# One Haar product in split float32r form for all 64 channels of the second batch instead of every other one

## The chip, the cores and the metric

The kernel runs on one core of one Trainium2 chip. The metric is the device time of one execution in microseconds (us), taken as the median of several runs. Engines are named as in the profile: PE is TensorE's matmul, PEld its weight load, DVE is VectorE, ACT is ScalarE, SP is SyncE, whose queue issues most of the DMAs.

## What is computed

The input x has 4 batches of 64 channels of 256x256 float32 pixels. Four layers follow one another. Layers 0, 1 and 3 are long convolutions, each with its own separable filter made by a small network; layer 2 is a Haar transform in two dimensions, a mixing over channels with soft thresholds, and the inverse transform.

```python
# layers 0, 1, 3
k = jnp.einsum('ijk,imk->ijmk', hx, hy)[0]          # separable filter of each channel
y = irfft2(rfft2(x) * rfft2(k) / fft_size)[..., :L, :L]
out = y + x * bias[:, None, None]
# layer 2
f1 = haar2d(x)
for i in range(2):
    f4 = jnp.einsum('bchw,oc->bohw', f1 * v[i], conv_w[i])
    acc = acc + jnp.sign(f4) * jax.nn.relu(jnp.abs(f4) - tau[i])
y = haar2d(acc, inverse=True) + x
```

## The kernel before

**Convolutions as triangular matrix products.** The filters are separable, so each convolution of a 256x256 image is a product with a Toeplitz matrix along the columns and one along the rows. `toeplitz` loads such a matrix from a padded row of the filter in DRAM. `contract` (lines 189 and 190) does one side of one channel: for each of the two halves of 128 output rows one 128x256 and one 128x128 float32 matmul (a product with a zero quarter left out). `first` runs it and copies the PSUM result out on ACT (line 198, tiles `pa` to `a`); `second` runs the other side and adds the bias term on DVE (line 211, tiles `py` to `y`).

**Haar transform along the rows and down the columns.** After layer 1 a channel lies in `sd`, a ring of 8 channels. `pairs` and `levels` do the transform along the rows on DVE (lines 256, 257, 266, 267), `levels` for 4 channels at once in three steps. `down` does the transform down the columns as one product with a 128x128 matrix of Haar signs on PE, giving tile `pz`; ACT copies it to `co` (line 293) and SP stores it in DRAM (`coef`). There are two forms of `down`:

- Plain: one float32 product of `hbt` with the channel's `sd`, 512 columns (line 289).
- In parts, for channels in `in_parts`: `split` rounds the channel to float32r on ACT (line 277) and subtracts the rounded values on DVE (line 278), so that the two float32r tiles in `sp` add up to the channel. `down` then does two float32r products with `hbr` into the same PSUM bank (line 285). The matrix holds only signs[...]. `sp` has one buffer.

**Mixing and the way back.** `mixing` works on 64 groups of 4 rows of coefficients. Per group: four float32 products 128x256 (line 334, tile `px`, two PSUM buffers of two banks); the scale v on the way out of PSUM, for all but the last batch 4 of 16 slices on DVE (line 351) and 12 on ACT (line 353); absolute value and sign on ACT (lines 359, 360); threshold, product and sum on DVE (lines 361, 366, 370). `inverse` does the inverse transforms (`rows`, `cols`, lines 387 to 415) and layer 3's convolution for two channels out of three. The rest are put off and run by `convolution` beside the last batch's mixing.

**Order.** Nothing runs at once: every stage of every channel or group is put on a list with a tick (`at`, `stream`), the list is sorted, and the instructions are emitted in this order. A scheduler then gives each engine its own order, which it follows strictly. The convolutions of batch b+1 run beside the mixing and the inverse of batch b: `spread` deals 64 channels over the ticks, so that some ticks have a channel and some have none. For the second batch (b+1 = 1) these are ticks 64 to 145, with 64 channels; for the third and fourth batch the channels lie closer, 64 in 72 ticks. Ticks with no channel are called empty below. In the mixing of the first batch they come every four or five ticks (15 while its 64 groups run), in that of the second batch every nine (7 while its groups run).

`convolutions` gets `in_parts` as a range. Batches 0, 2 and 3 have all channels in it, batch 1 every other one.

Of the kernel before, what the change touches and what calls it, by code (L numbers as in the profile page):

```python
# [16 lines left out]
B, C, S, EMB, ORD = 4, 64, 256, 33, 64  # L17
# [20 lines left out]
def conv_seq_kernel(ctx, tc, x, fz, fw, bias, decay, haar, haar_row, factors, vt, taut, wmix, out):  # L38
# [138 lines left out]
    def toeplitz(layer, c, name):  # L177

        t = tp.tile([P, 2, S], F32, name=name, tag="toep")
        nc.sync.dma_start(t, ap(pads[layer], c * 2 * ROW, [[1, P], [ROW, 2], [1, S]]))  # L180
        return t

    def bank(name):
        return psm.tile([P, 2, S], F32, name=name, tag="mm")
# [7 lines left out]
    def first(b, st, key, layer, new):  # L192
        def run(c):
            s = st[c]
            ps = bank(f"p{new}_{b}_{c}")
            contract(ps, s[key], s[layer][:, 0, :])
            a = io.tile([P, 2, S], F32, name=f"{new}_{b}_{c}", tag="mid")
            nc.scalar.copy(a, ps)  # L198
            s[new] = a

        return run

    def second(b, st, key, layer, res, new, tag, ahead=None):
        def run(c):
            s = st[c]
            if ahead is not None:
                s[ahead] = toeplitz(ahead, c, f"t{ahead}_{b}_{c}")
            ps = bank(f"p{new}_{b}_{c}")
            contract(ps, s[key], s[layer][:, 1, :])
            y = io.tile([P, 2, S], F32, name=f"{new}_{b}_{c}", tag=tag, bufs=BUFS[tag])  # L210
            nc.vector.scalar_tensor_tensor(y, s[res], bsb[:, layer, c : c + 1], ps, ALU.mult, ALU.add)  # L211
            s[new] = y

        return run
# [12 lines left out]
    def at(tick, place, run, unit):  # L227
        events.append((tick, place, len(events), run, unit))

    def stream(stages, ticks):  # L230

        for unit, tick in enumerate(ticks):
            for s, stage in enumerate(stages):
                if stage is not None:
                    at(tick + s, -s, stage, unit)

    def convolutions(b, ticks, in_parts=(), border=None):


        st = {}  # L240

        def after(tick, n):
            return tick if border is None or tick < border or n < C // 4 - 2 else border + 3 * (tick - border)

        def load(c):
            xt = io.tile([P, 2, S], F32, name=f"x_{b}_{c}", tag="in", bufs=3)
            nc.sync.dma_start(xt, x[b, c].rearrange("(k p) w -> p k w", p=P))
            st[c] = {"x": xt, 0: toeplitz(0, c, f"t0_{b}_{c}")}

        last_second = second(b, st, "a1", 1, "y0", "y1", "res")  # L250

        def pairs(c):
            last_second(c)
            v = st.pop(c)["y1"].rearrange("p k (w e) -> p k w e", e=2)
            t = sd[:, c % 8]
            nc.vector.tensor_add(t[:, :, 0, :], v[:, :, :, 0], v[:, :, :, 1])
            nc.vector.tensor_sub(t[:, :, 1, :], v[:, :, :, 0], v[:, :, :, 1])
            nc.scalar.dma_start(keep[b][c], t)

        def levels(steps):  # L260
            def run(n):
                t = sd[:, n % 2 * 4 : n % 2 * 4 + 4]
                for step in steps:
                    v = t[:, :, :, 0, :].rearrange("p c k (w e) -> p (c k) w e", e=2 * step)
                    even, odd = v[:, :, :, 0], v[:, :, :, step]
                    nc.vector.tensor_sub(odd, even, odd)  # L266
                    nc.vector.scalar_tensor_tensor(even, even, 2.0, odd, ALU.mult, ALU.subtract)  # L267

            return run

        parts = {}

        def split(c):

            w = parts[c] = mx.tile([P, 2, 2, S], F32R, name=f"sp_{b}_{c}", tag="sp", bufs=1)
            t = sd[:, c % 8].rearrange("p k e w -> p k (e w)")
            nc.scalar.copy(w[:, 0], t)  # L277
            nc.vector.tensor_tensor(w[:, 1], t, w[:, 0].bitcast(F32), ALU.subtract)  # L278

        def down(c):  # L280
            ps = bank(f"pz_{b}_{c}")
            flat = "p k w -> p (k w)"
            if c in in_parts:
                for i in range(2):
                    nc.tensor.matmul(
                        ps.rearrange(flat), hbr, parts[c][:, i].rearrange(flat), start=(i == 0), stop=(i == 1)
                    )
            else:
                nc.tensor.matmul(
                    ps.rearrange(flat), hbt, sd[:, c % 8].rearrange("p k e w -> p (k e w)"), start=True, stop=True  # L290
                )
            t = io.tile([P, 2, S], F32, name=f"co_{b}_{c}", tag="co", bufs=BUFS["co"])
            nc.scalar.copy(t, ps)
            nc.sync.dma_start(coef[b][:, c].rearrange("k p w -> p k w"), t)

        stream(
            [load, first(b, st, "x", 0, "a0"), second(b, st, "a0", 0, "x", "y0", "y", ahead=1), first(b, st, "y0", 1, "a1"), pairs],
            ticks,
        )
        for n in range(C // 4):  # L300
            end = ticks[4 * n + 3] + 4
            for s, steps in enumerate([(1,), (2, 4), (8, 16, 32, 64)]):
                at(after(end + 1 + s, n), 1, levels(steps), n)
            for j in range(4):
                if 4 * n + j in in_parts:
                    at(after(end + 3 + j, n), 2, split, 4 * n + j)
                at(after(end + 4 + j, n), 2, down, 4 * n + j)
        return after(ticks[-1] + 11, C // 4 - 1)
# [128 lines left out]
    def convolution(which, ticks):  # L437

        for (b, c), tick in zip(which, ticks):
            st = {}  # L440

            def load(c, b=b, st=st):
                u = io.tile([P, 2, S], F32, name=f"v_{b}_{c}", tag="in", bufs=3)
                nc.sync.dma_start(u, late[b, c])
                st[c] = {"u": u, 2: toeplitz(2, c, f"t2_{b}_{c}")}

            for s, stage in enumerate([load, *last(b, st)]):
                at(tick + s, -s, stage, c)


    def spread(begin, end, n=C):
        return [begin + i * (end - begin - 1) // (n - 1) for i in range(n)]
# [19 lines left out]
    ready = convolutions(0, range(C), in_parts=range(C))  # L472
    ahead = C
    start = ready + 3
    for b in range(B):
        mixing(b, start, 12 if b + 1 < B else 6)
        end = start + groups + 3
        if b + 1 < B:
            ready = convolutions(b + 1, spread(ahead, end + 2), in_parts=range(0, C, 2 if b == 0 else 1), border=end)
        else:  # L480
            convolution(
                [(i, c) for i in range(B - 1) for c in sorted(put_off)], spread(start - 2, end + 2, (B - 1) * len(put_off))
            )
        inverse(b, end, put_off if b + 1 < B else ())

        start = max(end + C, ready + 3)
        ahead = start - 3
# [111 lines left out]
```

## Time and profile before

| | |
|---|---|
| runs (us) | 2994.05, 2999.53, 2990.19; median 2994.05 |
| profiled execution | 2994.63 us, its span 2992.8 us |
| PE busy | 2929.2 us, 98% of the span, 16950 instructions |
| PEld busy | 2610.1 us, 87% |
| DVE busy | 2535.0 us, 85% |
| ACT busy | 2147.1 us, 72% |
| TensorE clock granted | full in all 40 slices |
| DMA | 649.72 MB, mean 217 GB/s |

Read by the first and last `px` product, the stretches of the span are: filters and convolutions of the first batch up to 452 us; mixing of the first batch beside convolutions of the second, 452 to 867; inverse of the first beside the rest of the second's convolutions, 867 to 1094; the same two stretches for the next batch, 1094 to 1543 and 1543 to 1774, and the next, 1774 to 2222 and 2222 to 2452; the last mixing, 2452 to 2729, and its inverse to the end. Busy time counts an instruction from its start to its end as recorded; instructions of one engine overlap somewhat, and a float32 matmul of the program stands in the trace as two instructions.

### The profile page before, as it was taken

The page shows a single profiled execution, that of the slowest core. Times are in us where ns is not written, and L with a number is a line of the kernel's source. Part 1 is how long each engine was busy: PE and PEld are TensorE (multiplying, and loading weights), DVE is VectorE, ACT ScalarE, POOL GpSimd, SP SyncE. Part 2 cuts the span into 40 slices and gives each one's busy share as a digit, 9 for nine tenths or more (in the row PEclk, how much of TensorE's full clock was granted, in tenths as well). Part 3 has the DMA queues.
Part 4 walks back from the last instruction along what each step waited for, and adds up shares of the span by engine and source line. Part 5 has one row for each costly group of instructions (what it writes and reads, how often), then busy time and mean ns, then how long its engine had stood idle before and what let it go on. Part 6 is the DMA issues. An engine that isn't in the chain of part 4 may idle for free. (4 is left out here: it accounts for less than half of the span.)

```text
span 2992.8 us, 51867 instructions
## 1 busy us (share of the span) xinstructions
PE 2929.2 (98%) x16950; PEld 2610.1 (87%) x16950; DVE 2535.0 (85%) x4544; ACT 2147.1 (72%) x4973; POOL 0.2 (0%) x4
## 2 busy tenths in 40 slices
PE   7999999999999999999999999999999999999999
PEld 6899988888888888888888988888888988888998
DVE  4766778999988879999989879999998889998776
ACT  1333337989876658889886658989886768887554
POOL 0000000000000000000000000000000000000000
PEclk9999999999999999999999999999999999999999
DMA  5877776676667876666677876676677887777776
GB/s 146 250 233 230 229 232 207 206 206 199 204 196 245 247 216 202 206 210 201 207 212 241 253 222 198 209 212 202 205 210 234 254 239 229 229 233 220 211 212 186
DMA packets 562496, 649.72 MB, mean 217 GB/s; under 512 B 44369, under 2 KB 447412, under 8 KB 562100
## 3 DMA queue, kind: packets, MB, share of 16 engines
q1 hardware_dynamic: 446132, 494.94, 57.9%
q10 hardware_dynamic: 116096, 151.46, 14.1%
q8 instruction: 137, 2.24, 0.3%
q14 instruction: 131, 1.07, 0.1%
HBM read 426.77 MB, written 219.48 MB: 216 GB/s over the span
## 5 line engine op out<-in xcount | busy, mean ns | idle before, releaser
L189 PE MATMUL py<-t,a 128*128 128x256 f32 x3072 | 923.1, 382 | 19.2 <-ACT a L198 12.3
L198 ACT COPY a<-pa 128x512 f32<-128x512 f32 x768 | 472.4, 617 | 440.6 <-PE pa L190 305.7
L190 PEld LDWEIGHTS py<-t,a 128*128 128x128 f32 x3072 | 583.4, 190 | 79.3
L353 ACT ACTIVATE f<-px,vt 128x64 f32<-128x64 f32 x2688 | 588.8, 351 | 87.7 <-DVE f L351 81.8
L190 PE MATMUL py<-t,a 128*128 128x128 f32 x3072 | 590.1, 274 | 0.0
L189 PEld LDWEIGHTS py<-t,a 128*128 128x128 f32 x3072 | 491.0, 191 | 78.2 <-ACT a L198 35.7
L334 PE MATMUL px<-wb,f 128*128 128x256 f32 x2048 | 503.5, 381 | 16.7 <-ACT f L353 16.7
L334 PEld LDWEIGHTS px<-wb,f 128*128 128x128 f32 x2048 | 362.6, 191 | 62.1 <-ACT f L353 26.7
L361 DVE TENSOR_TENSOR mag<-mag,vt 128x1024 f32<-128x1024 f32 x256 | 312.2, 1220 | 30.9 <-ACT mag L359 28.8
L366 DVE SCALAR_TENSOR_TENSOR mag<-mag,f 128x1024 f32<-128x1024 f32 x256 | 311.9, 1218 | 3.8 <-DVE sd L267 0.3
L397 ACT CAST w<-pw 128x512 fp32r<-128x512 f32 x256 | 150.4, 587 | 227.9 <-PE pw L395 215.1
L189 PE MATMUL pa<-t,y 128*128 128x256 f32 x1024 | 306.9, 382 | 1.7 <-DVE y L211 1.4
L189 PE MATMUL pa<-t,x 128*128 128x256 f32 x1024 | 305.6, 380 | 1.3 <-issue 1.3
L359 ACT ACTIVATE mag<-f 128x1024 f32<-128x1024 f32 x256 | 284.3, 1110 | 18.7 <-DVE z L370 6.8
L387 ACT COPY zc<-z 128x512 f32<-128x512 f32 x256 | 282.4, 1103 | 2.0 <-ACT w L397 0.8
L360 ACT ACTIVATE f<-f 128x1024 f32<-128x1024 f32 x256 | 274.0, 1070 | 12.1 <-DVE sd L266 5.9
L211 DVE SCALAR_TENSOR_TENSOR y<-x,bsb,py 128x512 f32<-128x512 f32 x256 | 190.3, 743 | 57.8 <-PE py L190 49.9
L189 PE MATMUL pa<-t,u 128*128 128x256 f32 x772 | 232.8, 383 | 3.2 <-PE pu L407 3.2
L411 DVE SCALAR_TENSOR_TENSOR t<-r,pu 128x512 f32<-128x512 f32 x256 | 175.1, 684 | 64.1 <-PE pu L407 60.6
L278 DVE TENSOR_TENSOR sp<-sd,sp 128x512 fp32r<-128x512 f32 x224 | 153.9, 687 | 83.0 <-ACT sp L277 81.3
L190 PEld LDWEIGHTS pa<-t,x 128*128 128x128 f32 x1024 | 194.6, 190 | 26.3
L190 PEld LDWEIGHTS pa<-t,y 128*128 128x128 f32 x1024 | 194.5, 190 | 26.3
(67 smaller groups left out, 4449.0 us busy)
## 6 DMA issues: line engine op xcount, KB each, us to landing
t<-pad SPq DMA_DIRECT2D x768, 256.0 KB, 4.0
x<-in_x SPq DMA_DIRECT2D x256, 256.0 KB, 3.9
keep<-sd ACTq DMA_DIRECT2D x256, 256.0 KB, 3.0
coef<-co SPq DMA_DIRECT2D x256, 256.0 KB, 3.2
f<-coef SPq DMA_DIRECT2D x256, 256.0 KB, 4.0
r<-keep SPq DMA_DIRECT2D x256, 256.0 KB, 3.3
out_y<-y ACTq DMA_DIRECT2D x256, 256.0 KB, 3.7
late<-u ACTq DMA_DIRECT2D x63, 256.0 KB, 2.7
```

The source lines that it names most:

```text
L189: nc.tensor.matmul(ps[:, m, :], src[:, 0, m * P : (m + 1) * P], t[:, ::-1], start=True, stop=False)
L190: nc.tensor.matmul(ps[:, m, P:], src[:, 1, m * P : (m + 1) * P], t[:, : P - 1 : -1], start=False, stop=True)
L198: nc.scalar.copy(a, ps)
L211: nc.vector.scalar_tensor_tensor(y, s[res], bsb[:, layer, c : c + 1], ps, ALU.mult, ALU.add)
L334: nc.tensor.matmul(ps[:, h, q, :], f[:, q, h * P : (h + 1) * P], wb.rearrange("p r n -> p (r n)"), start=True, stop=True,)
L353: nc.scalar.mul(f4[:, j], px[:, j], scale(g, 0)[:, j : j + 1])
L359: nc.scalar.activation(mag, f4, AF.Abs)
L360: nc.scalar.activation(f4, f4, AF.Sign)
L361: nc.vector.tensor_sub(mag, mag, over(g, 1, 16))
L366: nc.vector.scalar_tensor_tensor(mag, mag, 0.0, st[g]["f4"], ALU.max, ALU.mult)
L387: nc.scalar.copy(a, z[:, :, :, c].rearrange("p h (i k) -> p h k i", k=2))
L411: nc.vector.scalar_tensor_tensor(t, st[c]["r"], 0.5, ps, ALU.mult, ALU.add)
```

## The change

The second batch's channels all go in parts: `in_parts` becomes `range(C)` for every batch. For 32 channels (the odd ones of the second batch) the plain product is replaced by a split and two float32r products. The branch for the plain form stays in the code but is not used any more.

```diff
@@ -476,7 +476,7 @@
         mixing(b, start, 12 if b + 1 < B else 6)
         end = start + groups + 3
         if b + 1 < B:
-            ready = convolutions(b + 1, spread(ahead, end + 2), in_parts=range(0, C, 2 if b == 0 else 1), border=end)
+            ready = convolutions(b + 1, spread(ahead, end + 2), in_parts=range(C), border=end)
         else:
             convolution(
                 [(i, c) for i in range(B - 1) for c in sorted(put_off)], spread(start - 2, end + 2, (B - 1) * len(put_off))
```

The parts of `convolutions` that the choice steers:

```python
        def split(c):
            w = parts[c] = mx.tile([P, 2, 2, S], F32R, name=f"sp_{b}_{c}", tag="sp", bufs=1)
            t = sd[:, c % 8].rearrange("p k e w -> p k (e w)")
            nc.scalar.copy(w[:, 0], t)
            nc.vector.tensor_tensor(w[:, 1], t, w[:, 0].bitcast(F32), ALU.subtract)
...
                if 4 * n + j in in_parts:
                    at(after(end + 3 + j, n), 2, split, 4 * n + j)
                at(after(end + 4 + j, n), 2, down, 4 * n + j)
```

## The prediction

> **What bounds the kernel now.** I read the page's busy shares first, then busy time by stretch, the two forms of the product `pz`, the matmul starts in the timeline, and who waits for whom. The page:
>
> ```profile
> PE 2929.2 (98%) x16950; PEld 2610.1 (87%) x16950; DVE 2535.0 (85%) x4544; ACT 2147.1 (72%) x4973; POOL 0.2 (0%) x4
> ```
>
> PE looks full. Since matmuls overlap in the record, I took the start-to-start spacing: in steady rows a float32 256-column instruction starts 0.216 us after the one before, a 128-column one after 0.110. Whatever exceeds the usual spacing of the same pair of lines I call lost; it is 10.8 us in the first mixing stretch, 14.3 in the second, 13.8 in the third, 11.1 in the last. So PE bounds every stretch, with 2 to 4% lost. Busy time by stretch (first, second, last mixing; the columns after the length are PE, PEld, DVE, ACT):
>
> ```profile
> 452.00:867.00 415.00, 409.32 (x2210) 354.94 (x2209) 377.60 (x654) 368.99 (x1055) 0.00 (x0) 1.00 0.68 204
> 1094.00:1543.00 449.00, 440.62 (x2456) 391.96 (x2454) 411.32 (x718) 389.29 (x1094) 0.00 (x0) 1.00 0.68 205
> 2452.00:2729.00 277.00, 272.21 (x1461) 239.86 (x1461) 268.85 (x316) 235.20 (x558) 0.00 (x0) 1.00 0.79 231
> ```
>
> The reader is to see that VectorE (91%) and ScalarE (89%) are close behind PE in the stretch where the change adds to both.
>
> The waits in the first and, in the second fence, the second mixing stretch:
>
> ```profile
> PE px L334 <- ACT f L353: 2.2, 3, 1.1
> ```
>
> ```profile
> PE px L334 <- ACT f L353: 5.1, 7, 0.8
> ```
>
> In the second stretch, where every channel goes in parts already, PE stops seven times for ScalarE to empty a `px` buffer: once for each of its seven empty ticks.
>
> **What the Trainium skill says.** "Perfetto Trace Analysis", section Identifying the Most-Contended Engine, warns that matmul busy share is no good measure and points to weight loads; here these are 87%, and the spacing decides. "TensorE: Matmul & The Clock Gate", section Back-to-back issue gap, gives N/2.4 + 2.5 ns, 216 ns for 512 columns. The trace agrees for one recorded float32 instruction only if it is counted as two passes (256 columns in 216 ns, 512 in 430). For float32r the trace has 0.314 and 0.233 us for the two products of 512 columns, more than the page's 0.216, so I use the trace. "VectorE: DVE Perf Modes", section The TRN2 errata, gives (N+151)/0.96, 691 ns, for a float32 `tensor_tensor` of 512; the subtraction of line 278 takes 687, and back to back the next starts after 0.60.
>
> **The change part by part.**
>
> *1. Cheaper products, 32 of them.* Plain form, then form in parts, each with what PE starts next:
>
> ```profile
> 603.48 1.02 PE L289 MATMUL pz<-sd,hbt 128*128 128x512 f32 x2
> ...
> 604.34 0.59 PE L189 MATMUL py<-t,a 128*128 128x256 f32 x2
> ```
>
> ```profile
> 1287.91 0.71 PE L285 MATMUL pz<-sp,hbr 128*128 128x512 f32 x2
> 1288.46 0.59 PE L189 MATMUL pa<-t,y 128*128 128x256 f32 x2
> ```
>
> PE is held 0.86 us in one, 0.55 in the other. The medians over all rows give 0.431 + 0.430 = 0.861 against 0.314 + 0.233 = 0.547: 0.314 us a channel. All 32 plain products lie between 452.7 and 1009.5 us; line 289 has 50 instructions, so 25 channels, in the first mixing stretch and 14, so 7 channels, in the inverse behind it. **PE's own work falls by 25 x 0.314 = 7.8 and 7 x 0.314 = 2.2, together 10.0 us.** Weight loads stay two a channel.
>
> *2. 32 splits.* Each is a cast on ScalarE (0.52 us when the next follows at once: starts 1290.95 and 1291.47) and a subtraction on VectorE (0.60: starts 1292.50 and 1293.10). In the first mixing that is 25 x 0.52 = 13.0 us and 25 x 0.60 = 15.0. It is hidden only while these engines stay ahead of PE. Over the shortened 415 - 7.8 = 407 us VectorE would have (377.6 + 15.0) / 407 = 96% and ScalarE (369.0 + 13.0) / 407 = 94%. The last mixing runs at 97% of VectorE and loses 11.1 of 277 us. In the inverse stretch VectorE has 186.6 of 227 us, and 7 splits there cost nothing: PE's work covers them, and were this cover gone they would cost at most 7 x 0.60 = 4.2.
>
> *3. Waits added.* `sp` has one buffer, so the cast for one channel waits for both products of the channel before, now one tick earlier instead of two; behind it on ScalarE stand the `px` copies and the `pa` copies, for which PE waits. In 224 splits now, 192 of them with the next channel split too, no cast is listed as waiting for `pz`; 0 us. The casts wait for VectorE's line 267 (4.8 us, six times), and the products for no subtraction of line 278. I take 0; lower bound 0, since no wait is removed, upper bound 25 x 0.2 us (those six waits average 0.8, one in four) = 5. DMAs are the same in number and size; SP's order differs in a few places, whose waits I take as nothing, within ±1 us.
>
> *4. The order.* In the built program of the changed kernel PE's order outside the second batch's convolutions stays as it was, inside it does not. In the second mixing each empty tick makes a knot: the `px` of one group directly followed by the first half of the next group's. Seven knots there; the timeline at one:
>
> ```profile
> 1281.72 1.89 PE L334 MATMUL px<-wb,f 128*128 128x256 f32 x8
> 1284.41 1.13 PE L334 MATMUL px<-wb,f 128*128 128x256 f32 x4 [0.80 <-ACT f L353]
> ```
>
> The line shows PE standing until ScalarE has emptied the older buffer. Such a knot loses 0.96 + 0.10 there and 0.25 + 0.07 + 0.32 + 0.10 within the next 21 us, 1.8 us in all. The first mixing has six knots now, one in its start-up; the other five lose 0.3, 0.7, 0.2, 1.1 and 0.9 us, 0.64 each. **In the changed program it has fourteen, one at nearly each empty tick.** The 10.8 us lost now are 2.4 at the start-up (to 480 us), 3.2 at five knots, 5.2 at smaller stops around other empty ticks, which the new knots replace. After: 2.4 + 14 x s. With s = 0.64 (knots of this stretch) 11.4; with s = 1.8 (knots with all channels split, but nine ticks apart) 27.6. I choose 1.2, the middle: the same splits as there, but in a looser knot (the changed order has mostly 4.9 + 4.9 + 1.7 us of PE work between the four `px` starts, the second mixing's 4.9 + 4.3 + 1.7). That is 19.2 us, 8.4 more than now; bounds +0.6 and +16.8.
>
> *Sum.* -10.0 + 0 + 0 + 8.4 = **-1.6 us** against the profiled execution's own 2994.6 (span 2992.8 and 1.8 around it), so 2993.0. The median of the runs is 0.6 below that execution: **2992.5 us**. With both ends of s, -9.4 to +6.8, with the cast's wait up to +12. A measurement of this kernel can tell about 0.3%, 9 us, from no change, so even the whole gain of 10.0 would hardly show.
>
> **The rivals.**
>
> *A. The full 10 us.* The knots cost no more than the stops that they replace, and ScalarE and VectorE keep ahead: 2994.05 - 10 = 2984. For it: the present knots of 0.64 us. Against it: all 14 would have to, with VectorE at 96%. Chance 0.14.
>
> *B. Slower: ScalarE sets the pace of the first mixing.* Per nine ticks there are 9 groups and 7 channels. ScalarE needs 9 x (12 x 0.196 + 0.96 + 0.95 = 4.26) + 7 x (3 x 0.47 for copies, 0.52 for the cast, 0.37 for a DMA issue = 2.30) = 54.4 us; PE needs 9 x 8 x 0.216 + 7 x (5.22 + 0.55) = 55.9. The stretch now takes 415 / 64 x 9 = 58.4. Knots come every 4.5 ticks, so what ScalarE owes after one may not be paid before the next; an owed `px` copy holds PE, and PE's late `pa` then holds ScalarE. If ScalarE is kept to 90% of its time, nine ticks take 60.4, 64 groups 14 us more than now; with 2.2 from the inverse stretch +12, 3006. It decides from a loss of 2.0 us a knot (2.4 + 27.5 = 29.9, 19 above now). For it: two engines within 4% of PE. Against it: around the knot at 1284 ScalarE has only some 0.9 us idle in 27, so it can do 97%. Chance 0.14.
>
> *C. Not what it says*, a float32r pair no cheaper than the plain product: the two fences of step 1 exclude it.
>
> **How the numbers follow.** Likeliest case, part of the gain eaten by the knots: 0.72, at 2992.5, its own range 2986 to 3001. A has 0.14, some of which measures as no change, B 0.14. Faster than 2985: 0.10, slower than 3003: 0.14, between: 0.76. The range for 8 in 10 takes in s from 0.64 to 1.8 and a few us of run-to-run spread (2990 to 3000 now): 2984.5 to 3003.
>
> **What would show it.** In the profile after, line 289 is gone and line 285 has 512 instructions, with PE spaced 0.55 us over a pair. VectorE's and ScalarE's busy sums in the first mixing rise by some 13 to 17 us each. `px` waits for line 353 there fourteen times instead of three, and the time lost rises from 10.8 to about 19. The inverse behind it shortens by 2 us, everything later stays. Wrong would be: a first mixing longer than 415 us (B), or shorter than 408 (A); casts of line 277 waiting for `pz` (step 3); or a change after 1094 us.

## The result and the profile after

The changed kernel takes 2989.05 us (median of 14 runs, 2987.12 to 2992.38), the kernel before in the same comparison 2994.07 (14 runs). The ratio is 0.9985, 95% interval 0.9978 to 0.9992: 5 us faster. That is inside the 0.3% that I had called no change, but the interval, from this many runs, leaves out 1. The number hides two larger ones, a gain of about 13 us and a loss of about 8, and the experiments below take them apart as far as they go.

The head of the page after:

```profile
span 2987.4 us, 51999 instructions
...
PE 2919.9 (98%) x16950; PEld 2610.5 (87%) x16950; DVE 2551.9 (85%) x4576; ACT 2156.5 (72%) x5005; POOL 0.2 (0%) x4
```

PE has the same number of instructions and 9.3 us less busy time; DVE and ACT have 32 instructions more each, which are the splits. Now the instructions of tile `pz` after (duration minimum/median/maximum in ns, first and last start):

```profile
L285 PE MATMUL pz<-sp,hbr x512: 387/474/586, 86.1 to 2364.7; 128*128 128x512 f32 x171
```

Line 289 is gone, line 285 has 512 instructions. Busy time by stretch after (length, PE, PEld, DVE, ACT), from the first to the last `px` product of the first mixing:

```profile
458.00:865.00 407.00, 396.95 (x2183) 350.94 (x2183) 387.46 (x672) 375.44 (x1077) 0.00 (x0) 1.00 0.68 204
```

VectorE is busy 95% of it, ScalarE 92%, PE 98%. The page's share for ScalarE over the span, 72%, says nothing of this. And the waits in this stretch after:

```profile
PEld px L334 <- ACT f L353: 9.7, 11, 1.3
ACT f L353 <- DVE f L351: 5.8, 11, 0.9
...
PE px L334 <- ACT f L353: 5.3, 11, 0.9
...
PEld pz L285 <- DVE sp L278: 2.6, 4, 1.2
```

PE waits eleven times instead of three for ScalarE to empty a `px` buffer. The last line is new: the weight load of a pair's second product waits for the subtraction of its split (the product itself once, 0.9 us).

Measured by the starts of the matmuls, as in the prediction, the first mixing was 409.7 us long and is 406.5. It begins with its first `px` product, at 457.5 us in the kernel before; the 452 us from which the windows ahead of the result count lie 5.5 us earlier. On that scale the prediction's 415 us became 411.8, so neither of its signs (longer than 415, shorter than 408) came. All other stretches differ by 1.5 us or less either way; the inverse of the first batch is 1.2 shorter.

### The profile page after: what moved, and what is told of

Same layout as the page of the kernel before. It is cut to its first block, busy times and chain, and to the rows that moved or that the text cites. A ratio compares the mean times of both kernels' runs of the same rounds, so it can differ in the third digit from the quotient of the medians.

```text
span 2987.4 us, 51999 instructions
## 1 busy us (share of the span) xinstructions
PE 2919.9 (98%) x16950; PEld 2610.5 (87%) x16950; DVE 2551.9 (85%) x4576; ACT 2156.5 (72%) x5005; POOL 0.2 (0%) x4
## 5 line engine op out<-in xcount | busy, mean ns | idle before, releaser
L189 PE MATMUL py<-t,a 128*128 128x256 f32 x3072 | 923.3, 382 | 17.8 <-ACT a L198 8.6
L360 ACT ACTIVATE f<-f 128x1024 f32<-128x1024 f32 x256 | 273.2, 1067 | 13.1 <-DVE sd L257 5.7
L278 DVE TENSOR_TENSOR sp<-sd,sp 128x512 fp32r<-128x512 f32 x256 | 176.6, 690 | 92.6 <-ACT sp L277 91.9
```

Source lines behind the costliest of these rows:

```text
L189: nc.tensor.matmul(ps[:, m, :], src[:, 0, m * P : (m + 1) * P], t[:, ::-1], start=True, stop=False)
L360: nc.scalar.activation(f4, f4, AF.Sign)
```

## The experiments

In the tables and texts below the length of the first mixing runs from its first to its last `px` product, and "lost" is PE time beyond the usual spacing of the same pair of lines. "To the second mixing" runs from the first `px` product of the first mixing to that of the second, so it takes in the inverse behind. Outside the second batch's convolutions and what runs beside them all kernels but the last two have the same program. The lengths, the lost time and the knots are read from one profiled execution each. The kernels were compared with the kernel before in several groups, in which its median was 2994.07 to 2995.33, so the ratios are the better comparison.

| kernel | us | ratio to before (95% interval) | first mixing, us | lost in it, us | to the second mixing, us | knots in the first mixing: full, short |
|---|---|---|---|---|---|---|
| before | 2994.07 | 1 | 409.7 | 10.8 | 642.1 | 5, 1 |
| changed | 2989.05 | 0.9985 (0.9978 to 0.9992) | 406.5 | 17.8 | 637.8 | 14, 0 |
| no splits for odd channels | 2982.31 | 0.9958 (0.9944 to 0.9971) | 402.5 | 13.8 | 632.9 | 3, 10 |
| splits alone | 2994.54 | 1.0000 (0.9992 to 1.0008) | 411.5 | 12.7 | 644.1 | 7, 7 |
| none in parts | 3008.10 | 1.0043 (1.0030 to 1.0055) | 419.4 | 10.3 | 655.0 | 4, 2 |
| cast only | 2988.78 | 0.9979 (0.9972 to 0.9986) | 406.3 | 17.7 | 636.4 | 14, 0 |
| subtraction only | 2983.47 | 0.9962 (0.9950 to 0.9975) | 404.2 | 15.7 | 635.0 | 5, 8 |
| ten on ScalarE | 2988.46 | 0.9976 (0.9967 to 0.9985) | 403.5 | 14.6 | 636.7 | 2, 4 |
| cast on VectorE | 2988.17 | 0.9975 (0.9966 to 0.9985) | 404.0 | 13.3 | 637.2 | 1, 4 |
| eleven on ScalarE | 2984.08 | 0.9962 (0.9949 to 0.9974) | 401.0 | 10.8 | 633.0 | 5, 9 |
| before, eleven on ScalarE | 2995.44 | 1.0005 (0.9997 to 1.0013) | 411.0 | 12.2 | 643.6 | 1, 3 |
| eleven in three mixings | 2972.34 | 0.9924 (0.9912 to 0.9937) | 400.2 | 10.1 | 632.0 | 5, 9 |
| the same, seven at the end | 2991.58 | 0.9989 (0.9981 to 0.9997) | 400.5 | 10.4 | 631.9 | 5, 9 |

A knot is, as in the prediction, the `px` of one group directly followed by `px` of the next. The traces have two kinds. At a full knot the eight `px` instructions of a group are followed by four of the next, as in the prediction's example; at a short one by two. The numbers of knots in the expectations put both together and differ from the table by a few. Full knots cost: entering the next group at them PE lost 2.5 us at the five of the kernel before and 8.2 at the fourteen of the changed one. Short ones cost little in most kernels (0.04 us at seven, 0.2 at nine), but 1.8 us at ten without odd splits and 2.6 at eight with the subtraction only.

**The gain alone: no splits for odd channels.**

```diff
-                if 4 * n + j in in_parts:
+                if 4 * n + j in in_parts and (b != 1 or j % 2 == 0):
...
-                        ps.rearrange(flat), hbr, parts[c][:, i].rearrange(flat), ...
+                        ps.rearrange(flat), hbr, parts[c - c % 2 if b == 1 else c][:, i].rearrange(flat), ...
```

> The changed kernel, but the odd channels of the second batch have no split: their two float32r products read the parts of the even channel before (part of the computation is left out: the column transform of 32 channels is that of a neighbour). PE's products are those of the changed kernel, VectorE's and ScalarE's work that of the kernel before. PE's order still has twelve knots in the first mixing. Load theory (what ate a part of the gain is the added splits): time lost on PE in the first mixing stays near 11 us, the product saving of about 13 us shows nearly whole, 2981 to 2983. Order theory (the knots cost, whatever the load): lost time 15 to 18 us, 2986 to 2989. If a pair saves only the 0.314 us of the prediction, load theory gives 2984.

12.3 us faster: inside the range of the load theory. The trace puts 9.2 us of it into the first mixing and the inverse behind it; the rest lies in stretches whose program is that of the kernel before, so 2 or 3 us between two medians are not read as an effect here. The lost time is 13.8 us, 3.0 above before. The order theory is not refuted by it: this order has only three full knots where the changed kernel has fourteen, so not only the load differs.

Why the products save 13 us and not the 10.0 of the prediction is in the starts around a pair in the changed kernel:

```profile
539.18 0.38 PE L190 MATMUL pa<-t,x 128*128 128x128 f32 x2
539.32 0.71 PE L285 MATMUL pz<-sp,hbr 128*128 128x512 f32 x2
539.87 0.59 PE L189 MATMUL pa<-t,y 128*128 128x256 f32 x2
```

From the start of the two line-190 instructions to line 189 behind the pair it is 0.69 us. In the kernel before the same two instructions started at 603.26 and line 189 behind the plain product at 604.34: 1.08 us. The difference is 0.39, not 0.31. The pair's own 0.55 us are as predicted, but its first product starts 0.031 us after the last instruction ahead of it (median over the first mixing), where the plain product starts 0.112 behind the same line. Behind `px` it is 0.03 against 0.216. Summed with these medians over the 24 plain products between the first and the last `px` of the first mixing that is 10.2 us, over the 7 of the inverse 2.8; one more lies just ahead of the mixing.

**The load alone: splits that nobody needs.**

```diff
-            if c in in_parts:
+            if c in in_parts and (b != 1 or c % 2 == 0):
                 for i in range(2):
```

> All channels of the second batch are split, but the odd ones use the plain float32 product and leave their parts unread. PE's work is that of the kernel before, VectorE's and ScalarE's that of the changed kernel; the order has twelve knots in the first mixing. Load theory: as PE is slower by 13 us than in the changed kernel, the engines beside it keep ahead somewhat better, lost time 13 to 17 us against 10.8, 2996 to 3000. Order theory: the same 15 to 18 us lost, 2998 to 3001. If splits are fully hidden and knots cost nothing: 2994.

No change in the run time: the third case, below what either theory gave. In the trace the first mixing is 1.8 us longer, with 1.9 us more lost. So the splits cost at most that while the plain products keep PE slow. Beside the cheap products the same splits cost 4.9 us by the trace (637.8 against 632.9). The two halves of the change do not add up: a gain of 12.6 and 0 apart, 4.5 together by the ratios (their intervals leave 8 give or take 5 us), 9.2 and a loss of 2.0 apart, 4.3 together by the traces.

**The change run backwards: none of the second batch in parts.**

```diff
-            ready = convolutions(b + 1, ..., in_parts=range(C), border=end)
+            ready = convolutions(b + 1, ..., in_parts=range(C) if b else (), border=end)
```

> The second batch has no channel in parts: the change run the other way, 32 more plain products and 32 fewer splits. The order has few knots (as before). If a plain product costs PE 0.40 us more than a pair, counting that the pair starts right behind the matmul ahead of it: +13 us, and lost time falls by at most the few us that the 32 splits of the kernel before cost: 3003 to 3007. If only the 0.314 us of the prediction: 3000 to 3004. If the step from none to half nets as much as that from half to all: 2999.

13.5 us slower by the medians (12.9 by the ratio; 12.8 in the trace from the first mixing to the second): at the top of the first theory or 1 us above it, and out of the other two. The first 32 channels in parts thus bring the whole product saving and the second 32 only 5 us of it. Lost time is 10.3, 10.8 and 17.8 us with none, half and all in parts: it stays flat and then rises, as the number of full knots does: 4, 5 and 14.

**Which half of the split: cast only, subtraction only.** For the odd channels of the second batch one half of the split is left out and both products read what there is (their lines in `down` are left out here).

```diff
-            nc.vector.tensor_tensor(w[:, 1], t, w[:, 0].bitcast(F32), ALU.subtract)
+            if b != 1 or c % 2 == 0:
+                nc.vector.tensor_tensor(w[:, 1], t, w[:, 0].bitcast(F32), ALU.subtract)
```

> The changed kernel, but of the odd channels' splits in the second batch only the cast on ScalarE is kept; both products read the rounded part (the remainder is left out of these 32 channels). PE's products as in the changed kernel, ScalarE's work as there, VectorE's as before; fourteen knots. Known: without any odd split 2982.3, with both halves of it 2989. If the late px copies on ScalarE are the cause: nearly all of the loss comes back, 2987 to 2989. If it is VectorE: 2982 to 2984. If only both together hurt: 2983 to 2985, and the next run too.

```diff
-            nc.scalar.copy(w[:, 0], t)
-            nc.vector.tensor_tensor(w[:, 1], t, w[:, 0].bitcast(F32), ALU.subtract)
+            if b != 1 or c % 2 == 0:
+                nc.scalar.copy(w[:, 0], t)
+                nc.vector.tensor_tensor(w[:, 1], t, w[:, 0].bitcast(F32), ALU.subtract)
+            else:
+                nc.vector.tensor_tensor(w[:, 1], t, t, ALU.subtract)
```

> The counterpart: of the odd channels' splits only the subtraction on VectorE is kept (the channel minus itself, so these 32 channels lose their coefficients), and both products read its result. ScalarE's work as before, VectorE's as in the changed kernel; thirteen knots. If VectorE is the cause: 2987 to 2989. If ScalarE: 2982 to 2984. If only both together: 2983 to 2985.

With the cast only, PE runs all its 16950 instructions in the order of the changed kernel and loses 17.7 us, against 17.8. So with the order held, taking away the added subtractions gives nothing back in the mixing (1.4 us from the first mixing to the second): the higher busy share of VectorE did not mark the cause.

The subtraction alone is nearly as fast as no split by its median; its five runs all lie below the fastest with the cast only, though the ratios' intervals overlap a little. That points to ScalarE's 0.52 us a channel. It is not shown, for two reasons. Of the 5.3 us between the two medians the traces have only 1.4 from the first mixing to the second, the part in which the programs differ. And the order is not the same: five full knots instead of fourteen. Here is how long PE waited for the `px` copies, first with the cast only, then with the subtraction only (the edits move the line numbers: 335 and 337 are line 334, 354 and 356 line 353):

```profile
PE px L335 <- ACT f L354: 5.1, 9, 1.5
```

```profile
PE px L337 <- ACT f L356: 4.9, 6, 1.1
```

The wait is as long in total with no cast added. No run here holds the order and changes ScalarE's work alone, so the cast and the full knots stay two causes that were not separated.

**Taking work off ScalarE.** Of the 16 slices in which `px` leaves PSUM, 12 go over ScalarE.

```diff
-        mixing(b, start, 12 if b + 1 < B else 6)
+        mixing(b, start, (10 if b == 0 else 12) if b + 1 < B else 6)
```

> The changed kernel with 10 instead of 12 of the 16 px slices on ScalarE in the first mixing (6 on VectorE): ScalarE -25 us, VectorE about +9 us there (64 x 128 more columns). Five knots instead of fourteen. If ScalarE's px copies and the knots are what stops PE, px waits for line 353 vanish nearly and lost time falls from 17.8 to 11 or less: 2980 to 2983. If VectorE (busy 95% of the stretch already) is what paces it: lost time stays or grows, 2989 to 2995.

Between the two. The waits of the first mixing:

```profile
PEld pz L285 <- DVE sp L278: 6.3, 10, 1.2
...
PE pz L285 <- DVE sp L278: 3.0, 5, 0.9
...
PE px L334 <- ACT f L353: 0.9, 2, 0.7
```

`px` hardly waits for ScalarE any more, as the first theory has it; instead `pz` waits for VectorE's subtraction. The inverse behind loses 10.0 us (7.9 in the changed kernel, 6.2 before), 2.1 of them in one stop of PE for a cast of line 277, which itself waited for VectorE's line 267; after this stop the granted clock was at half for 3.4 us. With 11:

```diff
-        mixing(b, start, 12 if b + 1 < B else 6)
+        mixing(b, start, (11 if b == 0 else 12) if b + 1 < B else 6)
```

> The changed kernel with 11 instead of 12 px slices on ScalarE in the first mixing: ScalarE -12.5 us, VectorE +4.3 us there, thirteen knots. Ten slices gave 2988.5. If the two engines trade off smoothly around the balance: 2986 to 2988.5. If ScalarE's pacing is what counts and the order with its knots does not: 2985 to 2987. If the knots of the order count: as the changed kernel, 2989.

Below all three: 2984.08 us, 10.8 us lost, which is the number of the kernel before. `px` waits 1.7 us for ScalarE and `pz` 1.1 for VectorE; neither engine is late for long. It keeps most of the product saving (11.4 us by the ratio, 9.2 in the trace). Of the 7.0 us less lost than in the changed kernel 5.1 are at the knots, of which nine are now short and only five full; a full one costs about the same in both (0.58 and 0.59 us). So less work on ScalarE and a better order came together here too. The remaining route, the cast itself on VectorE:

```diff
-            nc.scalar.copy(w[:, 0], t)
+            (nc.vector.tensor_copy if b == 1 else nc.scalar.copy)(w[:, 0], t)
```

> The changed kernel with the cast of all second-batch channels on VectorE instead of ScalarE: in the first mixing ScalarE has 49 x 0.52 = 25 us less, VectorE 49 casts more, by 0.3 to 0.6 us each (no such row in the trace; the subtraction takes 0.60) 15 to 29 us. If ScalarE is the cause and VectorE has room: 2983 to 2986. If VectorE is the tighter of the two: its sum reaches 400 to 415 us in a stretch of 403, so 2992 to 3003.

Between the two. A cast on VectorE shows 0.42 us (median), VectorE is busy 395.9 of 404 us in the first mixing. The mixing is 2.5 us shorter than in the changed kernel, the inverse behind it 1.8 longer with 9.9 us lost. Its order has few knots (one full, four short), and it is no faster than with ten slices.

**Is it the change, or just a better number?** Here the edit is made to the kernel before.

```diff
-        mixing(b, start, 12 if b + 1 < B else 6)
+        mixing(b, start, (11 if b == 0 else 12) if b + 1 < B else 6)
```

> The kernel before with 11 instead of 12 px slices on ScalarE in the first mixing. If eleven slices help by themselves: lost time there falls from 10.8 towards 6, 2989 to 2991. If they only take away what the added casts brought: 2993 to 2996.

No change: on the kernel before, eleven slices bring nothing. They only undo what the added splits and their order brought. Nor do fewer full knots with less work on ScalarE always make a kernel faster: this one has one instead of five, and loses more ahead of `py` (9.2 us instead of 5.7). The second and third mixing have had all channels in parts all along, so there the same should work:

```diff
-        mixing(b, start, 12 if b + 1 < B else 6)
+        mixing(b, start, 11 if b + 1 < B else 6)
```

> The changed kernel with 11 slices on ScalarE in the first three mixings. With 11 in the first alone: 2984.1. The second and third lose 13 us each, 7 of it px waiting for px behind ScalarE, and their order has four knots instead of seven. If ScalarE's copies cause that too: lost time there falls by 3 to 6 us each, 2972 to 2978. If VectorE, at 92% there, takes it back: 2982 to 2986.

2972.3 us, 0.76% below the kernel before: the version that beats both, as the first theory had it. The head of its page (of the fastest of its five runs), then the `px` waits in the second mixing, first of the changed kernel, then of this one:

```profile
span 2965.5 us, 51734 instructions
```

```profile
PEld px L334 <- ACT f L353: 7.8, 7, 1.2
PE px L334 <- ACT f L353: 5.0, 7, 0.8
```

```profile
PEld px L334 <- ACT f L353: 2.5, 7, 0.5
```

The matmuls' own wait is gone from the list; the second and third mixing lose 7.4 and 7.3 us instead of 13.1 and 12.9 and are 5.7 us shorter each. The order changed here too: one full and six short knots in each, with 1.5 us lost at them, instead of six and one with 6.8.

**One step too far: seven at the end.**

```diff
-        mixing(b, start, 11 if b + 1 < B else 6)
+        mixing(b, start, 11 if b + 1 < B else 7)
```

> As the run before, and in the last mixing 7 slices on ScalarE instead of 6, as VectorE is busy 97% of it: VectorE -4.3 us, ScalarE +12.5. Its order has about nineteen knots there instead of two. If VectorE bounds the last mixing: 2 to 5 us below the run before. If the knots and ScalarE's copies weigh more: 0 to 8 us above it.

The lines are against the run before. 19 us slower than that run, beyond the worst that I had given. The last mixing:

```profile
PEld px L334 <- ACT f L353: 21.5, 13, 3.2
PE px L334 <- ACT f L353: 16.7, 7, 2.8
```

It loses 32.8 us instead of 10.9, with `px` behind ScalarE in front, though ScalarE is busy only 244 of 293 us. Its order has seven full and eight short knots there instead of one full. At the full ones PE lost 21.0 us, at the short ones nothing. One of the seven:

```profile
2474.23 1.52 PE L334 MATMUL px<-wb,f 128*128 128x256 f32 x4 [1.97 <-ACT f L353]
2475.54 1.06 PE L189 MATMUL py<-t,a 128*128 128x256 f32 x2
...
2478.83 0.60 PE L189 MATMUL pa<-t,v 128*128 128x256 f32 x2
```

The granted clock, 0.96 over this stretch, is full except in seven spells of 3.4 us, where it is at half; here it is the spell from 2474.8 to 2478.3, in which instructions of one shape take 1.06 instead of 0.60 us a pair. Each spell begins after PE's stop at a full knot has begun, so the lower clock follows the stops and did not cause them. My estimate from these numbers is that it makes up 7 x 3.4 / 2 = 12 us of the loss. Whether the order or the copies make the stops was not separated here.

## Why the prediction was right or wrong

- **What bounds the kernel:** right. PE's own work set the time, and 98% busy did mean nearly full: of the first mixing 2.6% was lost before and 4.4% after.
- **Step 1, products:** the mechanism was right, the size was not. 0.314 us a channel should have been about 0.39 (behind line 190) to 0.50 (behind `px`): the term left out the start of the first product against the matmul ahead of it. Some 13 us instead of 10.0, which the kernel with none in parts shows (12.8 to 13.5, with about the same time lost). The prediction's rival of the full gain, and the bound on any gain, were built on 10.0.
- **Step 2, splits:** they are nearly hidden by PE's plain products (splits alone: no change in the run time), and less so when PE gets faster (4.9 us by the traces). The prediction priced them at nothing in the sum and let the knots stand for their effect. VectorE was named first, at 96%; but without the added subtractions, in the same order, the loss stayed (17.7 us). The busy sums in the first mixing rose by 12 us on VectorE and 8 on ScalarE, less than the 13 to 17 given as a sign.
- **Step 3, waits:** that no cast waits for `pz` held: the profile after lists none. That no product waits for a subtraction did not: PE lost 2.8 us in the first mixing between the two products of a pair (0.4 before), once 1.1 us at a stretch.
- **Step 4, order:** the built program had its fourteen knots, and the lost time rose from 10.8 to 17.8 us, close to the 19.2 forecast. That the total came so near is luck. A knot cost 0.59 us and not 1.2, which makes 8.2 us and not 16.8: the lower end, taken from the knots of this same stretch, was nearly right. The stops ahead of `py` and `pa`, which the new knots were to replace, stayed (6.7 us), and the 2.8 us within the pairs were not foreseen. Of the 7.0 us more that were lost, 4.7 are at knots and 2.4 within the pairs. Whether the knots need the added casts beside them was not separated: no run has fourteen full knots without the casts.
- **Sum:** -1.6 us forecast, -5.0 measured. The first mixing: -10.2 of products and +7.0 lost give the -3.2 of the trace. The inverse behind it: -2.8 and +1.7. The prediction's +8.4 was nearly the 8.7 of these two, for reasons that were right in part; its -10.0 was too small by 3.
- **Rivals:** A did not come: 7 us more were lost in the first mixing. Its 2984 is what the kernel with eleven slices took, in whose first mixing no more was lost than before. B named ScalarE, for whose copies PE does wait longer, but its size was wrong: 7 us more lost in the first mixing, not 19.

## What to carry to other kernels

When an engine that is full gets relief, work hidden beside it may come to light: measure the relief and the added load apart, then together, since here they did not add up. Do not pick the culprit by busy share: VectorE had the higher one, and leaving out its added work changed nothing. Ask of every such experiment whether it left the order of the instructions alone. Here only one did, and that one ruled a cause out; in the others load and order moved together. After making the full engine faster, rebalance the work beside it: with one slice in sixteen moved from ScalarE to VectorE the loss was gone, with two more than half of it was back.

## What the runs showed of the hardware

Two float32r products of 512 columns took 0.314 + 0.233 us on PE and started 0.03 us behind the float32 instruction ahead, where a float32 product started 0.11 or 0.22 us behind it. So behind line 190 a pair took 0.39 us less than one float32 product, which the spacing inside the pair does not show. ScalarE casts 128x512 float32 to float32r in 0.52 us back to back; VectorE's cast of the same shape shows 0.42 us in the trace.

Between the first 60 us and the end of the program, PE stood still for 1.97 to 2.75 us nine times in these traces (seven times with seven slices at the end, once each with ten slices and in the kernel before with eleven). Every time the granted clock was then at half for 3.4 us, beginning 2.3 to 3.5 us after the stop began. After the stops of up to 1.84 us it stayed full.
